# Two small maps made once on half of the matrix array, two groups of products moved in TensorE's order, and one load issued sooner

## The chip, the cores and the metric

The kernel runs on one core of a Trainium2 chip. A core has a matrix engine (TensorE, PE in the profile, with its weight loads as PEld), a vector engine (VectorE, DVE), a scalar engine (ScalarE, ACT), a general engine (GpSimd, POOL), and a queue engine that issues DMAs (SyncE, SP). The metric is the device time of one execution in microseconds (us), lower being better.

## The reference

x has 8 images of 256 channels and 64 x 64 pixels. Two layers follow each other, each of the form x + layer(group norm of x), with 32 groups of 8 channels.

Layer 0 computes, for every pixel, its own 3 x 3 filter:

```
x1, x2, x3 = 1x1 convolutions of gn(x): 32, 32 and 256 channels
h  = [x1, the 9 shifted copies of x2 (edge reflected)]      # 320 channels
h  = relu(bn(h));  h = relu(bn(cw1 h))                      # 32 channels
w  = cw2 h + cb2                                            # 9 taps for each of 32 groups
out[g, s] = sum over taps k of  w[g, k] * shift_k(x3[g, s]) # 8 channels s share a group's taps
```

Layer 1 adds two branches: an attention with 4 heads in which each pixel attends to its 7 x 7 neighbours (queries, keys with a position term, values, softmax over 49), and a dynamic convolution, in which x goes through two depthwise 3 x 3 convolutions for each of nine branches, and a softmax over the nine, from a 1x1 convolution of x, weights them.

## The kernel before

**Bands.** An image is cut into 8 bands of 8 rows (BAND = 512 pixels). Everything is done band by band, with channels or channel groups on the 128 partitions. One loop runs over g, from -12 to 63, and every g has 8 steps s. Step s does an eighth of layer 1's work on band g; beside it, layer 0 is done for a band 12 further on (AHEAD), since layer 1's normalisation needs a whole image of layer 0. While g is negative only layer 0 works: the *alone* stage, about 28 to 254 us of the profile. The rest, from 254 us on, is the *main* stage. In its last twelve bands, from about 3560 us, no layer 0 is left.

**Order.** The order of instructions on every engine is the order in which the program emits them (a manual schedule). A step has six places, each closed by `advance()`. `after(n, f)` emits f n places later. `steer` issues loads and starts chains of statistics. `beside(g, s)` returns two lists: `mid`, emitted behind the third place's beginning (the softmax's last scaling), and `end`, emitted behind the fifth. In the main stage a step puts on TensorE, in this order: weighted values of earlier scores (L735), scores (L691), the transposes of the probabilities before (ptp, L723), the first branch weights (pf, L813), what is in `mid`, the second pf, and what is in `end`.

**Buffers.** Results of TensorE lie in PSUM. Nearly all small users share the tag "gen" with five buffers, so that a group of matmuls waits until the buffer used five groups before has been emptied, mostly by ACT.

**Layer 0 for a band.** `small_maps` (called in `mid` of step 0) makes x1 and x2 from the loaded x (`xc`) with the scaled weights `w12s`: its 128 output partitions are x2 three times (one for each horizontal shift) and x1 once. Two products of 512 columns (L325) do it; in 32-bit floats each shows as two MATMULs. ACT copies them out, shifted by a column to each side (L332: three pieces of 32 partitions), with x1 (L335) and two reflected edge columns (L337, L338) into a tile of ten rows; POOL copies rows between neighbouring bands (L343 to L347). `value_maps` makes x3 (L357), copied out by ACT (L362) and stored to memory (L363) with two halves mt; in the main stage the first half is in `end` of step 0, the second in `mid` of step 1. `hidden_maps` starts a chain with the places `at`: hid for three vertical shifts t (ACT, L406), `conv` for t = 0 and 1, then for t = 2 (L417: 32-column products for four quarters of a band into `ph`), and a relu into h2n (ACT, L423). `tap_weights` makes three of the nine taps (pw, L435), and VectorE multiplies each with x3 rearranged by groups (`x3q`, loaded by L377, L381, L385): `prod`, L448. POOL adds the products to `xg` (x by groups, loaded by L393), L456; in the alone stage every third goes through TensorE instead (L469), and `combine` adds them on VectorE (L476). `take` takes statistics (L484) and stores the result x1 for layer 1 (L488).

**Statistics of the input.** `first_stats` loads x for bands of the next image into `xs`, a single buffer, at step 7, and takes its statistics (L283, VectorE) 16 places later in the alone stage, 9 later in the main stage. `scaled_weights` then makes w12s, w3s and, by products of one column (`through`), the biases.

**Dynamic sum.** `dynamic_sum` ends the dynamic convolution for a half of the channels: POOL adds two partial sums of exponentials (L824), VectorE takes reciprocals (L831 to L836), POOL multiplies and adds into `xr` (L841 to L843), and the band is stored.

Of the kernel before, what the change touches and what calls it, by code (L numbers as in the profile page):

```python
# [10 lines left out]
F32 = mybir.dt.float32  # L11
BF16 = mybir.dt.bfloat16
AF = mybir.ActivationFunctionType
# [5 lines left out]
P = 128  # L19
C = 256  # L20
NCT = C // P
H = W = 64
HW = H * W
R = 8
BAND = R * W
NB = H // R
# [4 lines left out]
REL = 32  # L31
# [29 lines left out]
AHEAD = NB + 4  # L61
AHEAD0 = AHEAD + NB + 1
# [24 lines left out]
def conv_layers_kernel(ctx: ExitStack, tc: tile.TileContext, ins: dict, out: bass.AP):  # L87
    nc = tc.nc
# [26 lines left out]
    par = load("par", [P, NPAR])  # L115
    chan = load("chan", [P, NCT, NCHAN], ins["chan"].rearrange("(t p) n -> p t n", p=P))
    rowp = load("rowp", [P, NROW], ins["rowp"].partition_broadcast(P))
    w12 = load("w12", [P, NCT, P], ins["w12"].rearrange("(t p) n -> p t n", p=P))
    w3 = load("w3", [P, NCT, C], ins["w3"].rearrange("(t p) n -> p t n", p=P))
    c1 = load("c1", [P, 3, REL])  # L120
    gq = load("gq", [P, P])
# [166 lines left out]
    def scaled_weights(b):  # L288

        im = images[b]  # L290

        def scale(sc, bi):
            im.w12s = w0.tile([P, NCT, P], F32, tag="w12s", name=f"w12s_{b}", bufs=1)
            im.w3s = w0.tile([P, NCT, C], F32, tag="w3s", name=f"w3s_{b}", bufs=1)
            for kt in range(NCT):
                nc.vector.tensor_scalar(im.w12s[:, kt], w12[:, kt], sc[:, kt : kt + 1], None, ALU.mult)
                nc.vector.tensor_scalar(im.w3s[:, kt], w3[:, kt], sc[:, kt : kt + 1], None, ALU.mult)
            after(5, lambda: through(bi))

        def through(bi):  # L300
            pb = ps.tile([P, 1 + NCT], F32, tag="gen", name=f"pb_{b}", bufs=5)
            for m, w in enumerate((w12, w3[:, :, :P], w3[:, :, P:])):
                for kt in range(NCT):
                    nc.tensor.matmul(
                        pb[:, m : m + 1], w[:, kt], bi[:, kt : kt + 1], start=(kt == 0), stop=(kt == NCT - 1)
                    )
# [12 lines left out]
    def small_maps(b, i):  # L319


        im = images[b]
        p12 = ps.tile([P, BAND], F32, tag="gen", name=f"p12_{b}_{i}", bufs=5)
        for kt in range(NCT):
            nc.tensor.matmul(p12, im.w12s[:, kt, :], im.xc[i][:, kt, :], start=(kt == 0), stop=(kt == NCT - 1))  # L325
        p12 = p12.rearrange("p (r c) -> p r c", r=R)
        t = im.x2[i] = w0.tile([P, HR, W], F32, tag="x2", name=f"x2_{b}_{i}", bufs=2)
        bias = im.bias
        for q, (dst, src) in enumerate(((1, 0), (0, 0), (0, 1))):
            n = W - (q != 1)  # L330
            s = slice(32 * q, 32 * q + 32)
            nc.scalar.activation(  # L332
                t[s, 1 : 1 + R, dst : dst + n], p12[s, :, src : src + n], AF.Identity, bias=bias[s, 0:1]
            )
        nc.scalar.activation(t[96:128, 0:R, :], p12[96:128], AF.Identity, bias=bias[96:128, 0:1])  # L335

        nc.scalar.activation(t[0:32, 1 : 1 + R, 0:1], p12[0:32, :, 1:2], AF.Identity, bias=bias[0:32, 0:1])  # L337
        nc.scalar.activation(  # L338
            t[64:96, 1 : 1 + R, W - 1 : W], p12[64:96, :, W - 2 : W - 1], AF.Identity, bias=bias[64:96, 0:1]
        )  # L340

        if i == 0:
            nc.gpsimd.tensor_copy(t[0:96, 0, :], t[0:96, 2, :])  # L343
        else:
            nc.gpsimd.tensor_copy(t[0:96, 0, :], im.x2[i - 1][0:96, R, :])
            nc.gpsimd.tensor_copy(im.x2[i - 1][0:96, R + 1, :], t[0:96, 1, :])
        if i == NB - 1:  # L347
            nc.gpsimd.tensor_copy(t[0:96, R + 1, :], t[0:96, R - 1, :])
# [471 lines left out]
    def dynamic_sum(b, i, ct, ex, oc):  # L820

        tot = ex[:, 1]
        xr = images[b].xr[i]
        nc.gpsimd.tensor_add(tot, tot, ex[:, 0])  # L824
        rec = w1.tile([P, BAND], F32, tag="rec", name=f"rec_{b}_{i}_{ct}", bufs=1)
        n = BAND // 2

        def quotient():


            nc.vector.tensor_scalar(tot, tot, 1.0, 1.0e37, ALU.add, ALU.min)  # L831
            nc.vector.reciprocal(rec[:, :n], tot[:, :n])
            after(3, second)

        def second():
            nc.vector.reciprocal(rec[:, n:], tot[:, n:])  # L836
            after(2, weigh)

        def weigh():

            nc.gpsimd.tensor_mul(tot, tot, rec)  # L841
            nc.gpsimd.tensor_mul(oc, oc, tot)
            nc.gpsimd.tensor_add(xr[:, ct], xr[:, ct], oc)  # L843
            if ct == NCT - 1:
                after(6, store)

        def store():
            nc.sync.dma_start(
                out=out[b].rearrange("(t p) n -> p t n", p=P)[:, :, i * BAND : (i + 1) * BAND], in_=xr
            )  # L850

        after(5, quotient)


    def beside(g, s):
# [51 lines left out]
        alone = g < 0  # L907
        if 0 <= g + AHEAD < B * NB:
            bq_, iq = divmod(g + AHEAD, NB)
            if s == 0:  # L910
                mid.append(lambda: small_maps(bq_, iq))
            if s == (2 if alone else 0):
                (mid if alone else end).append(lambda: value_maps(bq_, iq, 0))
            if s == (3 if alone else 1):
                mid.append(lambda: value_maps(bq_, iq, 1))
        if 0 <= g + AHEAD - 1 < B * NB and s == (2 if alone else 1):
            at = (3, 7, 8, 12, 16) if alone else (5, 9, 12, 15, 17)
            end.append(lambda: hidden_maps(*divmod(g + AHEAD - 1, NB), at))
        if 0 <= g + AHEAD - 2 < B * NB and s in TAPS_AT[alone]:
            u = TAPS_AT[alone].index(s)  # L920
# [5 lines left out]
    def steer(g, s):  # L926
# [4 lines left out]
        n = g + AHEAD + 1  # L931
        if s == 2 and n % NB == 0 and 0 < n < B * NB:
            scaled_weights(n // NB)
        if s == 7 and g + AHEAD0 < B * NB:
            first_stats(*divmod(g + AHEAD0, NB), n=16 if g < -1 else 9)
        if s == 5 and 0 <= g + 1 < B * NB:
            bn, inx = divmod(g + 1, NB)
            xr = images[bn].xr[inx] = x_tile("xr", bn, inx)
# [10 lines left out]
    with tc.manual_schedule():  # L949
# [21 lines left out]
        for g in range(-AHEAD, B * NB):  # L971
            b, i = divmod(g, NB)
            for s in range(STEPS):
                ct, m = divmod(s, NT // 2)
                mid, end = beside(g, s)
                steer(g, s)
                if g >= 0:
                    nm = f"{b}_{i}_{ct}_{m}"
                    sco = score_tile(nm)
                    weighted = [(a, weighted_values(*a, pt, sco)) for a, pt in pending]  # L980
# [53 lines left out]
def _layout(inputs):  # L1034
# [1 line left out]
    a = {k.replace("L0_conv_", "a_").replace("L1_conv_", "b_"): np.asarray(v) for k, v in inputs.items()}  # L1036
    f = np.float32
    arr = {"x": a["x"].reshape(a["x"].shape[0], C, HW)}
    arr["w12"] = np.concatenate([a["a_w2"].T] * 3 + [a["a_w1"].T], axis=1)
    arr["w3"] = a["a_w3"].T  # L1040

    def branch(v):
# [15 lines left out]
    par[:, PB21] = np.concatenate([a["a_b2"]] * 3 + [a["a_b1"]])  # L1058
# [55 lines left out]
```

## Time and profile before

| what | before |
|---|---|
| time, median of 3 runs | 4217.34 us (4215.47 to 4221.78) |
| the profiled execution | 4217.1 us |
| its span in the trace | 4215.3 us |
| mean TensorE clock granted | 0.994 of full |
| TensorE busy | 4079.7 us, 97% of the span |
| VectorE, ScalarE, GpSimd busy | 3582.1, 3046.5, 2900.3 us |
| x written by ACT (L332, L335, L337, L338): one | 670 and 679, 679, about 265 ns |
| VectorE waiting for xs in the alone stage | 47.3 us in 9 places |

A row of the profile's groups reads: line, engine, operation, output <- inputs with partitions x elements, count | busy us, mean ns of one | idle time of the engine just ahead of them, and what ended it. A group's mean can be longer than the time between two starts, since matmuls are pipelined; the distance from start to start is then what one costs. A row of the timeline reads: start, length, engine, line, operation, and for a run of equal instructions their count. A window reads: its bounds and length, and for each engine its busy time and count, then the clock granted to TensorE, the busy share of DMA and GB/s.

### The profile page before, as it was taken

The numbers are of one execution on the slowest core, as the hardware profiler recorded it, in microseconds if no ns is written. First come the engines' busy times: TensorE is split into PE (matmuls) and PEld (weight loads), VectorE is DVE, ScalarE is ACT, GpSimd is POOL, SyncE is SP. The second block draws the span as 40 slices with busy tenths as digits, with TensorE's granted clock in tenths as the row PEclk, the third lists the DMA queues.
The fourth block names the chain that finished last, engine by engine and source line by source line (L and its number), as shares of the span: only waits on it lengthen the run. The fifth ranks groups of instructions, "written<-read, shape, count | busy, mean of one in ns | idle before, by whom it ended". The sixth has DMA issues, their size and how long they took to land.

```text
span 4215.3 us, 72044 instructions
## 1 busy us (share of the span) xinstructions
PE 4079.7 (97%) x25004; PEld 2134.8 (51%) x25004; DVE 3582.1 (85%) x7244; ACT 3046.5 (72%) x7598; POOL 2900.3 (69%) x1778
## 2 busy tenths in 40 slices
PE   5889999999999999999999999999999999999998
PEld 2445555555555555555555555555555555555554
DVE  5778988888898898888988888888988888977777
ACT  3367778777777777877778777777778777677776
POOL 3657777677776777767777767767777777744445
PEclk9999999999999999999999999999999999999999
DMA  7753334233243333333333333343333233111100
GB/s 219 187 141 101 79 91 106 70 95 98 68 102 95 82 95 85 88 95 95 80 86 104 78 98 88 76 104 88 78 89 89 63 95 77 34 45 39 38 28 21
DMA packets 381260, 367.91 MB, mean 87 GB/s; under 512 B 55392, under 2 KB 282720, under 8 KB 380640
## 3 DMA queue, kind: packets, MB, share of 16 engines
q1 hardware_dynamic: 377568, 358.68, 33.4%
q8 instruction: 199, 3.26, 0.3%
q10 hardware_dynamic: 3328, 4.62, 0.3%
q14 instruction: 165, 1.35, 0.1%
HBM read 261.48 MB, written 101.71 MB: 86 GB/s over the span
## 4 chain that ended last, share of the span: by engine, by line
PE 74%; DVE 12%; POOL 7%; ACT 3%; issue 2%; SPq 2%; DMA 1%; POOLq 0%; ACTq 0%; DVEq 0%
PE pf L813 34%; PE ptp L723 6%; PE sco L735 5%; PE pk L646 5%; PE sco L691 5%; PE p L357 4%; POOL xg L456 4%; DVE prod L448 4%; PE pq L625 3%; PE pv L551 3%; PE pvt L595 2%; PE p L325 2%; PE pw L435 2%; POOL ex L1010 2%; DVE acc L796 2%
## 5 line engine op out<-in xcount | busy, mean ns | idle before, releaser
L813 PE MATMUL pf<-yp,c_wfc 128*128 128x512 f32 x4096 | 1932.4, 595 | 9.3 <-ACT vc L569 4.3
L456 POOL TENSOR_TENSOR xg<-xg,prod 128x1024 f32<-128x1024 f32 x549 | 1203.4, 2192 | 127.4 <-DVE prod L448 104.4
L813 PEld LDWEIGHTS pf<-yp,c_wfc 128*128 128x128 f32 x4096 | 733.8, 191 | 702.7 <-issue 658.9
L1010 POOL TENSOR_TENSOR ex<-ex,ex 128x1024 f32<-128x1024 f32 x384 | 907.7, 2364 | 61.9 <-ACT ex L818 57.2
L818 ACT ACTIVATE ex<-pf 128x512 f32<-128x512 f32 x1024 | 607.2, 593 | 335.7 <-PE pf L813 167.1
L770 DVE SCALAR_TENSOR_TENSOR acc<-yp,c_chan,acc 128x504 f32<-128x504 f32 (+3 forms) x1104 | 766.6, 694 | 47.7 <-ACT acc L761 27.1
L841 POOL TENSOR_TENSOR ex<-ex,rec 128x512 f32<-128x512 f32 x128 | 163.4, 1277 | 914.7 <-DVE rec L836 881.7
L796 DVE SCALAR_TENSOR_TENSOR acc<-hid,c_chan,acc 128x504 f32<-128x504 f32 (+3 forms) x1024 | 758.2, 740 | 20.2 <-ACT acc L790 2.1
L448 DVE SCALAR_TENSOR_TENSOR prod<-pw,c_par,x3q 128x1040 f32<-128x1040 f32 x576 | 734.4, 1281 | 46.3 <-PE pw L435 26.0
L717 ACT ACTIVATE prob<-prob,tot 128x196 f32<-128x196 f32 x1024 | 411.6, 450 | 467.9 <-DVE tot L715 467.9
L700 DVE CUSTOM_DVE_ANT_0 prob<-sco,c_mask 128x196 f32<-128x196 f32 x1024 | 325.1, 355 | 292.5 <-PE sco L691 292.0
L708 ACT ACTIVATE prob<-prob,nmax 128x196 f32<-128x196 f32 x1024 | 462.2, 456 | 46.9 <-DVE nmax L700 46.4
L735 PEld LDWEIGHTS sco<-pt,vt 112*64 112x64 f32 x8160 | 279.2, 137 | 209.5 <-issue 71.4
L723 PE MATMUL ptp<-ident,prob 128*112 128x128 f32 x2044 | 341.3, 287 | 26.4 <-ACT prob L717 25.9
L735 PE MATMUL sco<-pt,vt 112*64 112x64 f32 x8160 | 349.7, 228 | 0.0
L725 ACT COPY pt<-ptp 112x512 f32<-112x512 f32 x511 | 296.2, 580 | 70.5 <-PE ptp L723 66.5
L723 PEld LDWEIGHTS ptp<-ident,prob 128*112 128x112 f32 x2044 | 204.1, 133 | 194.0 <-ACT prob L717 69.4
L691 PE MATMUL sco<-kb,qb 64*64 64x196 f32 x4096 | 294.5, 357 | 0.2 <-DVE kb L661 0.2
L551 PE MATMUL pv<-yp,c_wv 128*128 128x512 f32 (+2 forms) x576 | 251.4, 561 | 0.0
L646 PE MATMUL pk<-yp,c_wk 128*128 128x512 f32 (+2 forms) x576 | 245.0, 552 | 0.0
L625 PE MATMUL pq<-yp,c_wq 128*128 128x512 f32 x512 | 242.2, 596 | 2.3 <-DVE prod L448 2.3
L357 PE MATMUL p<-xc,w3s 128*128 128x512 f32 x512 | 242.7, 598 | 0.0
(136 smaller groups left out, 5288.6 us busy)
## 6 DMA issues: line engine op xcount, KB each, us to landing
x<-x3n SPq DMA_DIRECT2D x128, 264.0 KB, 2.1
x3q<-x SPq DMA_DIRECT2D x128, 264.0 KB, 7.1
xc<-in_x SPq DMA_DIRECT2D x64, 512.0 KB, 5.0
xg<-in_x SPq DMA_DIRECT2D x256, 128.0 KB, 4.8
x<-xg SPq DMA_DIRECT2D x256, 128.0 KB, 2.4
yp<-x SPq DMA_DIRECT2D x128, 256.0 KB, 3.3
xr<-x SPq DMA_DIRECT2D x64, 512.0 KB, 5.7
out_x<-xr SPq DMA_DIRECT2D x64, 512.0 KB, 3.1
```

What stands on the lines that cost most here:

```text
L448: nc.vector.scalar_tensor_tensor(prod[:, :, :RUN], pw[:, j, :RUN].unsqueeze(1).to_broadcast([P, SHARE, RUN]), par[:, PCB2 + k : PCB2 + k + 1],
L456: nc.gpsimd.tensor_add(im.xg[i], im.xg[i], rows(prod))
L646: nc.tensor.matmul(pk[:, :n], wk[:, kt, ct * P : (ct + 1) * P], im.yp[i][:, kt, a : a + n], start=(kt == 0), stop=(kt == NCT - 1),)
L691: nc.tensor.matmul(sco[half[t], h, :NKEY], qb[half[h], 2 * m + t].rearrange("p r c -> p (r c)"), kb[half[h], :, c0 : c0 + KW], start=True, ...
L708: nc.scalar.activation(prob[:, h, :NKEY], prob[:, h, :NKEY], AF.Exp, bias=nmax[:, h : h + 1], scale=-1.0, accum_out=tot[:, h : h + 1],)
L723: nc.tensor.transpose(ptp[:, h, ch], prob[:, h, ch * CHUNK : (ch + 1) * CHUNK], ident)
L735: nc.tensor.matmul(po[half[h], :, t * TQ : (t + 1) * TQ], im.vt[i + ch, m][:n, t, (2 * ct + h) * HD : (2 * ct + h + 1) * HD], pt[:n, h, ch ...
L770: nc.vector.scalar_tensor_tensor(o, yp[:, ct, ra + dr : rb + dr, ca + dc : cb + dc], chan[:, ct, CW1 + k : CW1 + k + 1], o, ALU.mult, ALU.add,
L796: nc.vector.scalar_tensor_tensor(o, hid[:, ra + dr : rb + dr, ca + dc : cb + dc], chan[:, ct, CW2 + k : CW2 + k + 1], o, ALU.mult, ALU.add,)
L813: nc.tensor.matmul(pf, wfc[:, kt, 2 * m + j, ct * P : (ct + 1) * P], images[b].yp[i][:, kt, PAD : PAD + R], start=(kt == 0), stop=(kt == N ...
L818: nc.scalar.activation(ex[:, j].rearrange("p (r c) -> p r c", r=R), pf, AF.Exp)
L1010: after(4, lambda ex=ex, exb=exb: nc.gpsimd.tensor_add(ex, ex, exb))
```

## The change

The weights `w12` now hold w2 and w1 once, 64 columns. `small_maps` issues four products in place of two: each of 64 output partitions and 256 pixels, the upper four rows of the band on partitions 0 to 63 and the lower four on 64 to 127. ACT's writing out is a function of its own, `write_maps`: from each half, the three shifted copies of x2 and x1, 8 pieces of 252 or 256 elements; the two reflected edge columns are now copied by POOL out of the finished tile. In the main stage the products are issued at the beginning of step 0, just ahead of L735; the writing stays in `mid` of that step.

The places of `hidden_maps` in the main stage become (5, 13, 14, 19, 21): `conv` for t = 0, 1 moves from the middle of step 3 to its end, `conv` for t = 2 from the middle of step 4 to its end; hid for t = 2 and the relu are later as well.

In the alone stage the load of xs is issued at step 3 in place of step 7, and its statistics are taken 40 places later in place of 16, so at the place where they were. On SP's queue it now stands behind the stores of x1 and ahead of the loads of xg and x3q.

In the last band's second half, the four POOL operations of `dynamic_sum` go to VectorE.

```diff
-    w12 = load("w12", [P, NCT, P], ins["w12"].rearrange("(t p) n -> p t n", p=P))
+    w12 = load("w12", [P, NCT, 2 * REL], ins["w12"].rearrange("(t p) n -> p t n", p=P))
...
-            for m, w in enumerate((w12, w3[:, :, :P], w3[:, :, P:])):
+            for m, to, w in ((0, 0, w12), (0, 64, w12), (1, 0, w3[:, :, :P]), (2, 0, w3[:, :, P:])):
                 for kt in range(NCT):
                     nc.tensor.matmul(
-                        pb[:, m : m + 1], w[:, kt], bi[:, kt : kt + 1], start=(kt == 0), stop=(kt == NCT - 1)
+                        pb[to : to + w.shape[2], m : m + 1], w[:, kt], bi[:, kt : kt + 1],
+                        start=(kt == 0), stop=(kt == NCT - 1),
                     )
...
-        p12 = ps.tile([P, BAND], F32, tag="gen", name=f"p12_{b}_{i}", bufs=5)
+
+        p12 = ps.tile([P, R // 2, W], F32, tag="gen", name=f"p12_{b}_{i}", bufs=5)
         for kt in range(NCT):
-            nc.tensor.matmul(p12, im.w12s[:, kt, :], im.xc[i][:, kt, :], start=(kt == 0), stop=(kt == NCT - 1))
-        p12 = p12.rearrange("p (r c) -> p r c", r=R)
+            for u in range(2):
+                nc.tensor.matmul(
+                    p12[64 * u : 64 * u + 64], im.w12s[:, kt, :],
+                    im.xc[i][:, kt, u * BAND // 2 : (u + 1) * BAND // 2],
+                    start=(kt == 0), stop=(kt == NCT - 1),
+                )
+        return lambda: write_maps(b, i, p12)
+
+    def write_maps(b, i, p12):
+        im = images[b]
         t = im.x2[i] = w0.tile([P, HR, W], F32, tag="x2", name=f"x2_{b}_{i}", bufs=2)
         bias = im.bias
-        for q, (dst, src) in enumerate(((1, 0), (0, 0), (0, 1))):
-            n = W - (q != 1)
-            s = slice(32 * q, 32 * q + 32)
+        for u in range(2):
+            r, o = u * R // 2, 64 * u
+            for q, (dst, src) in enumerate(((1, 0), (0, 0), (0, 1))):
+                n = W - (q != 1)
+                nc.scalar.activation(
+                    t[32 * q : 32 * q + 32, r + 1 : r + 1 + R // 2, dst : dst + n],
+                    p12[o : o + 32, :, src : src + n], AF.Identity, bias=bias[o : o + 32, 0:1],
+                )
             nc.scalar.activation(
-                t[s, 1 : 1 + R, dst : dst + n], p12[s, :, src : src + n], AF.Identity, bias=bias[s, 0:1]
-            )
-        nc.scalar.activation(t[96:128, 0:R, :], p12[96:128], AF.Identity, bias=bias[96:128, 0:1])
-
-        nc.scalar.activation(t[0:32, 1 : 1 + R, 0:1], p12[0:32, :, 1:2], AF.Identity, bias=bias[0:32, 0:1])
-        nc.scalar.activation(
-            t[64:96, 1 : 1 + R, W - 1 : W], p12[64:96, :, W - 2 : W - 1], AF.Identity, bias=bias[64:96, 0:1]
-        )
+                t[96:128, r : r + R // 2, :], p12[o + 32 : o + 64], AF.Identity, bias=bias[o + 32 : o + 64, 0:1]
+            )
+
+        nc.gpsimd.tensor_copy(t[0:32, 1 : 1 + R, 0:1], t[0:32, 1 : 1 + R, 2:3])
+        nc.gpsimd.tensor_copy(t[64:96, 1 : 1 + R, W - 1 : W], t[64:96, 1 : 1 + R, W - 3 : W - 2])
...
-        nc.gpsimd.tensor_add(tot, tot, ex[:, 0])
+        engine = nc.vector if (b, i, ct) == (B - 1, NB - 1, NCT - 1) else nc.gpsimd
+        engine.tensor_add(tot, tot, ex[:, 0])
...
-            nc.gpsimd.tensor_mul(tot, tot, rec)
-            nc.gpsimd.tensor_mul(oc, oc, tot)
-            nc.gpsimd.tensor_add(xr[:, ct], xr[:, ct], oc)
+            engine.tensor_mul(tot, tot, rec)
+            engine.tensor_mul(oc, oc, tot)
+            engine.tensor_add(xr[:, ct], xr[:, ct], oc)
...
-            if s == 0:
-                mid.append(lambda: small_maps(bq_, iq))
+            if alone and s == 0:
+                mid.append(lambda: small_maps(bq_, iq)())
...
-            at = (3, 7, 8, 12, 16) if alone else (5, 9, 12, 15, 17)
+            at = (3, 7, 8, 12, 16) if alone else (5, 13, 14, 19, 21)
...
-        if s == 7 and g + AHEAD0 < B * NB:
-            first_stats(*divmod(g + AHEAD0, NB), n=16 if g < -1 else 9)
+        if s == (3 if g < -1 else 7) and g + AHEAD0 < B * NB:
+            first_stats(*divmod(g + AHEAD0, NB), n=40 if g < -1 else 9)
...
                 if g >= 0:
+                    if s == 0 and g + AHEAD < B * NB:
+                        mid.append(small_maps(*divmod(g + AHEAD, NB)))
```

The host lays out the weights and the bias column of w12 to match (w2 and w1 once; b2 and b1 twice).

More of the change, by code (lines that the diff above doesn't have):

```diff
@@ L292, in scale @@
         def scale(sc, bi):
-            im.w12s = w0.tile([P, NCT, P], F32, tag="w12s", name=f"w12s_{b}", bufs=1)
+            im.w12s = w0.tile([P, NCT, 2 * REL], F32, tag="w12s", name=f"w12s_{b}", bufs=1)
             im.w3s = w0.tile([P, NCT, C], F32, tag="w3s", name=f"w3s_{b}", bufs=1)
@@ L1038, in _layout @@
     arr = {"x": a["x"].reshape(a["x"].shape[0], C, HW)}
-    arr["w12"] = np.concatenate([a["a_w2"].T] * 3 + [a["a_w1"].T], axis=1)
+    arr["w12"] = np.concatenate([a["a_w2"].T, a["a_w1"].T], axis=1)
     arr["w3"] = a["a_w3"].T
@@ L1057, in _layout @@
         par[:, at : at + 3] = branch(a[f"a_bn1_{n}"])
-    par[:, PB21] = np.concatenate([a["a_b2"]] * 3 + [a["a_b1"]])
+    par[:, PB21] = np.concatenate([a["a_b2"], a["a_b1"]] * 2)
     for at, n in ((PG2, "g"), (PB2, "b"), (PM2, "m"), (PV2, "v")):
```

## The prediction

> **What bounds the kernel now.** I read the page's busy time and its chain first, then the windows of the three stages, then the matrix engine's timeline through one ordinary band, then the groups, and last the waits and the chain of the stage in which layer 0 runs alone. From the page (engine busy; then the chain that ended last):
>
> ```profile
> PE 4079.7 (97%) x25004; PEld 2134.8 (51%) x25004; DVE 3582.1 (85%) x7244; ACT 3046.5 (72%) x7598; POOL 2900.3 (69%) x1778
> ...
> PE 74%; DVE 12%; POOL 7%; ACT 3%; issue 2%; SPq 2%; DMA 1%; POOLq 0%; ACTq 0%; DVEq 0%
> ```
>
> The windows (stretch, then busy time of PE, PEld, DVE, ACT, POOL) say where this holds:
>
> ```profile
> 28.00:254.00 226.00, 174.43 (x759) 87.97 (x758) 158.26 (x181) 92.96 (x167) 145.19 (x90) 0.92 0.76 203
> 254.00:3560.00 3306.00, 3266.88 (x20223) 1714.35 (x20224) 2892.60 (x5844) 2479.28 (x6178) 2394.85 (x1453) 1.00 0.35 88
> ```
>
> From 254 us on TensorE is busy 3266.88 of 3306 us, so a microsecond of TensorE taken out there is worth one, unless something else then comes too late; VectorE, at 2892.60, is next (88%). Ahead of 254 us no engine is full. The timeline of TensorE (start, length, line) over the seam of two steps:
>
> ```profile
> 1594.85 0.60 PE L595 MATMUL pvt<-ident,vc 128*112 128x128 f32 x4
> 1595.28 1.88 PE L325 MATMUL p<-xc,w12s 128*128 128x512 f32 x4
> 1597.00 1.88 PE L813 MATMUL pf<-yp,c_wfc 128*128 128x512 f32 x4
> 1598.72 1.88 PE L357 MATMUL p<-xc,w3s 128*128 128x512 f32 x4
> 1600.53 0.69 PE L735 MATMUL sco<-pt,vt 112*64 112x64 f32 x16
> 1601.14 0.58 PE L691 MATMUL sco<-kb,qb 64*64 64x196 f32 x8
> ```
>
> Nothing is idle: each group starts before the modelled end of the last. From start to start, L325 costs 1.72 us (1595.28 to 1597.00), as does pf; but p of L357 ahead of L735 costs 1.81 us. I read the extra 0.09 as the price of a change of tile shape (full array to 64 columns). The groups by form:
>
> ```profile
> L735 PE MATMUL sco<-pt,vt 112*64 112x64 f32 x7664 | 342.5, 229 | 0.0
> ...
> L332 ACT ACTIVATE x<-p,bias 32x504 f32<-32x504 f32 x128 | 85.7, 670 | 49.8 <-PE p L325 49.0
> ...
> L338 ACT ACTIVATE x<-p,bias 32x8 f32<-32x8 f32 x64 | 17.0, 265 | 0.8
> ```
>
> Sixteen L735 of 229 ns each fit in 0.69 us: they overlap. Their records start in pairs, one per column half, 6 to 7 ns apart, pair after pair 58 ns, where 64 columns alone at L325's rate (429 ns for 512) are 54 ns. So two column halves run together at almost full rate. L417's four column quarters do it less well: 134 ns a round, against 107 for 128 columns.
>
> [...] here L843 takes 1273 ns on POOL, and VectorE's L476 1210 ns for twice the elements, about 2.1 times.
>
> **Half-width maps.** Two logical products of 512 columns with the full array (4 instructions by 429 ns, 1.72 us) become four of 256 columns on half the array, 8 instructions in 4 pairs. A pair at L325's rate is 215 ns, so 4 make 0.86; with L735's overhead of 4 ns a pair, 0.87 us. That is 0.85 us saved a band, in the 52 bands made from 254 us on: **44.1 us**. Bounds: with L417's overhead (25%) 1.07 us, 33.7 us saved; without overlap nothing. Put ahead of L735 they share its shape, 64 columns: the change of shape comes ahead of L325 in place of L735, so its 0.09 neither goes nor comes twice. Twelve bands fall in the alone stage, where TensorE waits; nothing there. The additional bias product per image and smaller weight scaling are below 0.2 us each: nothing.
>
> **Their evacuation.** ACT wrote 2 x 670 + 680 + 680 + 2 x 265 = 3.2 us; now 8 pieces of 252 or 256 elements. From 8 elements (265 ns) to 504 (670) the slope is 0.82 ns an element, so 252 cost 0.47, eight 3.7 us: 0.5 us more. ACT is at 75% in this stage, so this costs only if a buffer comes late. In this band the writes ended at 1600.9 and their PSUM buffer was wanted again by TensorE at 1603.86 (pvt of the next step), the one behind it (pf's) at 1604.29 after release at 1601.5: slack 3.0 and 2.8 us. Measured from the step's first L735: the scores come 0.87 later (the maps are now ahead of them), so softmax's ACT work and with it the writes do too; the step's end comes 0.85 earlier; the writes take 0.5 longer. About 0.7 and 0.6 us are left: no stall in an ordinary band, but I allow **2 us lost** in all for bands of which this isn't true (0 to 15 are possible). POOL's two edge copies are 0.23 each at most (L345's price) in place of ACT's 2 x 0.265; behind them stand the halo copies, wanted only at the end of the next step.
>
> **Inner maps' conv.** Each of its two parts stood between full-array products (pf, L417, pk or pv). Now it is the last group ahead of L735, where a change of shape is paid anyway: three changes become two, twice a band: 2 x 0.095 x 53 bands = **10.1 us**. In each image's first band L417 also waited for ACT's hid (7 times 0.86 from 254 us on): the third hid was issued at place 12 and its products at 15; now at 14 and 19, five places on: **6.0 us**. The relu comes 4 places later; its h2n is wanted only by the tap weights of the loop's next band, so I take nothing; were it late, PE would wait about the 0.48 us of that operation.
>
> **Statistics' x in the alone stage.** The chain in time:
>
> ```profile
> 94.25 1.14 DVE xg L476
> ...
> 104.95 0.61 SPq L385
> 105.60 5.21 DMA xs<-in_x
> ...
> 111.44 0.68 DVE st L283
> 112.12 1.20 DVE prod L448
> 113.32 1.14 DVE xg L476
> ```
>
> A band's loop is: combine, 16 issues on SP's queue (0.6 each), the landing of xs, statistics, a product, combine. The waits for xs sum to 47.3 us in 9 places. xs is now issued behind the four stores of x1, ahead of x3n, xg and x3q; its buffer is free by then. But the product behind the statistics needs the last piece of x3q, issued just ahead of xs before and last now, and xs's 512 KB go through ahead of it. Before, that piece landed 1.1 to 1.8 us ahead of xs (109.61 and 110.81; 128.89 and 130.73). With the same bytes on the same queue I expect it to land about where xs did. What leaves the loop is then only the statistics, 2 x 0.68 us, now done while x3q is on its way: 8 rounds by 1.3 to 1.4, **11 us**. Bounds: 5 if x3q lands later than xs did, 25 if it lands where it did before.
>
> **The last weighted sum.** Four operations of 1.26 on POOL become VectorE's, about 0.66 each (half of L476's 1210 and a little): 4 x 0.6 = **2.4 us**, all behind the last product, VectorE being idle there.
>
> **Sum.** 44.1 + 10.1 + 6.0 + 11 + 2.4 - 2 = 71.6 us. The profiled execution took 4217.1 us (span 4215.3 and 1.8 around it), 0.2 below the median of 4217.34; 4217.1 - 71.6 = 4145.5, I say **4145 us**. A change under about 0.2%, 8.4 us, could not be told from none.
>
> **Rivals.** *The halves don't overlap* (two streams of 256 columns need more than L735's 64 showed): the 44.1 go, 4189 us; against it, pairs in L735 6 ns apart. *VectorE becomes the bound*: 2892.60 of 3306 busy, and the waits of L723 for prob, 24.45 us in 44 places, all lie in a band's last two steps, where VectorE is already late; TensorE's time taken out of step 0 comes out of VectorE's idle 2.78 us of step 1, which covers it in ordinary bands. If half of the 54 us of the first and third edits turn into such waits, 4172. *The wait for xs goes whole*, because x3q lands where it did: 14 more, 4131. *Slower*: the fixed part of a narrow write is larger than 8 elements show. The writes fit 3.7 + 0.6 us. At 0.72 us a piece they take 5.75, TensorE waits 1.4 us in step 1 of each of 52 bands, and all gain is gone; from 0.76 on, 4230. Against it, 128x196 writes on ACT take 450 to 456 ns and 32x8 265.
>
> **How the numbers follow.** The forecast as worked out 0.70, with its own range 4132 to 4158; xs's wait gone whole 0.10; VectorE 0.09; no overlap 0.07; slower 0.04. The two far cases are left out of the range for the most part: 4126 to 4174. Faster 0.95 (all but the slower case and a sliver), within 0.2% 0.02, slower 0.03.
>
> **What would show it.** Groups of the new maps of 0.87 us from start to start, with L735 behind them at once; eight narrow writes of 0.47; L417's new form ahead of L735 without its wait on hid; in the alone stage VectorE's statistics waiting for no DMA, its product waiting for x3q instead; in the tail VectorE where POOL stood. Wrong would make it: waits on ACT at pvt or p in step 1, longer waits of L723 for prob, or maps of 1.7 us.

## The result

The changed kernel takes 4152.41 us (median of 4 runs, 4151.30 to 4159.20) against 4217.48 for the kernel before (4 runs, 4215.47 to 4221.78): a ratio of 0.9848, 95% interval 0.9831 to 0.9865, 65 us. The profiled execution took 4152.64 us, its span 4150.9. The forecast was 4145. The page of the changed kernel (engine busy, then the chain that ended last):

```profile
PE 4022.6 (97%) x25292; PEld 2126.8 (51%) x25292; DVE 3591.9 (87%) x7248; ACT 3081.0 (74%) x7726; POOL 2923.0 (70%) x1902
...
PE 71%; DVE 14%; POOL 6%; ACT 5%; DMA 2%; issue 2%; SPq 1%; POOLq 0%; ACTq 0%; DVEq 0%
```

TensorE has lost 57 us of busy time, VectorE none, so VectorE's share rose from 85% to 87% and its part of the chain from 12% to 14%. The windows (stretch, busy time of PE, PEld, DVE, ACT, POOL, clock, DMA share, GB/s):

```profile
28.00:254.00 226.00, 179.72 (x840) 88.17 (x836) 164.70 (x195) 105.54 (x206) 150.78 (x114) 0.90 0.87 210
254.00:3560.00 3306.00, 3264.61 (x20825) 1738.08 (x20825) 2949.42 (x5940) 2544.42 (x6375) 2465.81 (x1584) 1.00 0.36 89
```

The first window now reaches 8 us into the main stage, whose first scores start at 246.30 us and not at 254.10. In the second, TensorE is as full as it was (3264.61 of 3306), and does more work in the same stretch. The timeline of TensorE over the seam of the same two steps as in the prediction:

```profile
1561.67 0.60 PE L607 MATMUL pvt<-ident,vc 128*112 128x128 f32 x4
1562.20 1.08 PE L328 MATMUL p<-xc,w12s 128*64 128x256 f32 x8
1563.11 0.64 PE L747 MATMUL sco<-pt,vt 112*64 112x64 f32 x16
1563.68 0.57 PE L703 MATMUL sco<-kb,qb 64*64 64x196 f32 x8
...
1566.39 0.60 PE L607 MATMUL pvt<-ident,vc 128*112 128x128 f32 x4
1566.82 1.88 PE L825 MATMUL pf<-yp,c_wfc 128*128 128x512 f32 x4
1568.54 1.88 PE L369 MATMUL p<-xc,w3s 128*128 128x512 f32 x4
```

The maps (L328) take 0.91 us from start to start, where L325 took 1.72. The weighted values behind them (L747) take 0.57 where 0.62 was usual: after a change of shape the second pair of a group starts about 0.05 us late (0.107 us after the first where L747 stands behind L369, 0.060 behind the maps), and now that falls to the maps (0.267, where their further pairs are 0.215 apart). Together 0.86 us for the maps: the forecast had 0.87. ACT's writes (groups by form):

```profile
L343 ACT ACTIVATE x<-p,bias 32x252 f32<-32x252 f32 x256 | 118.0, 461 | 44.4 <-PE p L328 37.0 <-DMA c_wk<-in_wk 5.0
```

461 ns a piece, against 470 forecast. I then took, for every step of every band, the time from its scores to those of the next step, and the difference to the kernel before. The medians by the image's band (bands 2 and 4 are like band 1), in us a step (the seam moves 0.86 from step 0 to step 7, since the maps are now ahead of the first scores):

```
band   step 0     1      2      3      4      5      6      7    whole band
  0    -0.98   0.00   0.00  -0.20  -1.13   0.25   0.30   0.86    -0.89
  1    -1.72   0.00   0.00  -0.20  -0.20   0.00   0.13   0.86    -1.11
  3    -1.72   0.00   0.00  -0.20  -0.20   0.09   0.64   0.86    -0.52
  5    -1.72   0.00   0.00  -0.20  -0.20   0.00   0.12   0.87    -1.11
  6    -1.72   0.00   0.00  -0.20  -0.19   0.37   0.00   0.86    -0.89
  7    -2.01   0.00   0.00  -0.20  -0.20   0.01   0.00   0.86    -1.53
```

Over 52 bands, steps 3 and 4 give 27.0 us, and steps 5 and 6 take 13.5 back. The rest of the 65: the first scores come 7.8 us sooner (8.7 without the maps that are now ahead of them), and from the last scores to the end of the span it is 19.4 us in place of 21.7. So the table raises two questions that the forecast did not raise: why moving the conv gave 0.4 us a band and not 0.2, and what takes it back in steps 5 and 6.

### The profile page after: what moved, and what is told of

It reads as the page before. It is cut to its first block, busy times and chain, and to the rows that moved or that the text cites. A ratio compares the mean times of both kernels' runs of the same rounds, so it can differ in the third digit from the quotient of the medians.

```text
span 4150.9 us, 72735 instructions
## 1 busy us (share of the span) xinstructions
PE 4022.6 (97%) x25292; PEld 2126.8 (51%) x25292; DVE 3591.9 (87%) x7248; ACT 3081.0 (74%) x7726; POOL 2923.0 (70%) x1902
## 4 chain that ended last, share of the span: by engine, by line
PE 71%; DVE 14%; POOL 6%; ACT 5%; DMA 2%; issue 2%; SPq 1%; POOLq 0%; ACTq 0%; DVEq 0%
PE pf L825 33%; PE ptp L735 5%; PE sco L747 5%; PE pk L658 5%; PE sco L703 5%; PE p L369 5%; DVE prod L460 4%; PE pq L637 4%; POOL xg L468 3%; PE pvt L607 2%; PE pv L563 2%; DVE acc L808 2%; PE pw L447 2%; DVE acc L782 2%; POOL ex L1026 2%
## 5 line engine op out<-in xcount | busy, mean ns | idle before, releaser
L825 PE MATMUL pf<-yp,c_wfc 128*128 128x512 f32 x4096 | 1930.5, 595 | 10.6 <-ACT vc L581 5.0
L782 DVE SCALAR_TENSOR_TENSOR acc<-yp,c_chan,acc 128x504 f32<-128x504 f32 (+3 forms) x1104 | 766.2, 694 | 42.3 <-ACT acc L773 21.7
L747 PEld LDWEIGHTS sco<-pt,vt 112*64 112x64 f32 x8160 | 283.8, 137 | 182.3 <-issue 51.7
L735 PE MATMUL ptp<-ident,prob 128*112 128x128 f32 x2044 | 341.7, 287 | 31.2 <-ACT prob L729 30.5
L747 PE MATMUL sco<-pt,vt 112*64 112x64 f32 x8160 | 347.0, 227 | 0.0
L735 PEld LDWEIGHTS ptp<-ident,prob 128*112 128x112 f32 x2044 | 203.9, 133 | 201.4 <-issue 77.7
L369 PE MATMUL p<-xc,w3s 128*128 128x512 f32 x512 | 244.4, 601 | 0.0
```

What stands on the lines that cost most here:

```text
L369: nc.tensor.matmul(p3, im.w3s[:, kt, mt * P : (mt + 1) * P], im.xc[i][:, kt, :], start=(kt == 0), stop=(kt == NCT - 1),)
L735: nc.tensor.transpose(ptp[:, h, ch], prob[:, h, ch * CHUNK : (ch + 1) * CHUNK], ident)
L747: nc.tensor.matmul(po[half[h], :, t * TQ : (t + 1) * TQ], im.vt[i + ch, m][:n, t, (2 * ct + h) * HD : (2 * ct + h + 1) * HD], pt[:n, h, ch ...
L782: nc.vector.scalar_tensor_tensor(o, yp[:, ct, ra + dr : rb + dr, ca + dc : cb + dc], chan[:, ct, CW1 + k : CW1 + k + 1], o, ALU.mult, ALU.add,
L825: nc.tensor.matmul(pf, wfc[:, kt, 2 * m + j, ct * P : (ct + 1) * P], images[b].yp[i][:, kt, PAD : PAD + R], start=(kt == 0), stop=(kt == N ...
```

## The experiments

**Each part alone.** Three kernels: the half-width maps alone, the moved conv alone (the line with `at` in the kernel before), and the sooner load of xs alone.

```diff
 # conv_only, in the kernel before
-            at = (3, 7, 8, 12, 16) if alone else (5, 9, 12, 15, 17)
+            at = (3, 7, 8, 12, 16) if alone else (5, 13, 14, 19, 21)
 # xs_only, in the kernel before
-        if s == 7 and g + AHEAD0 < B * NB:
-            first_stats(*divmod(g + AHEAD0, NB), n=16 if g < -1 else 9)
+        if s == (3 if g < -1 else 7) and g + AHEAD0 < B * NB:
+            first_stats(*divmod(g + AHEAD0, NB), n=40 if g < -1 else 9)
 # maps_only: the changed kernel with these two, and the engine of the last dynamic sum, put back
```

> The kernel before with the half-width maps alone (made ahead of weighted values, written out in the old place). If TensorE's time saved is passed on: 52 bands by 0.855 us (914 ns for the maps and 50 ns less for the weighted values behind them, against 1719) less some 4 us of waits for buffers in step 0, so about 40 us faster, 4177 us. If the waits for VectorE in a band's steps 5 to 7 already eat the gain of this edit by itself: 30 us faster or less, 4188 or more.

> The kernel before with the moved conv alone. The prediction's own count (one change of shape less a part, 0.095 each, and no wait for hid): 16 us faster, 4201. If going from 32 columns to 64 costs nothing, as the trace of the changed kernel suggests, two changes go for each part, 0.2 us: 21 us and 6.5 for the wait, less what comes back as waits for VectorE in steps 5 and 6; 20 to 27 us faster, 4190 to 4197.

> The kernel before with the sooner load of xs in the alone stage alone. If the last piece of x3q now lands where xs landed and only the statistics leave the loop: 9 us faster, 4208. If the wait for the transfer were really shorter: 20 us or more, 4197 or less.

Measured, beside a kernel before of 4216.80:

| kernel | median us | ratio, 95% interval | change |
|---|---|---|---|
| maps alone | 4174.24 | 0.9901 (0.9888 to 0.9915) | -42.6 |
| conv alone | 4203.22 | 0.9969 (0.9957 to 0.9981) | -13.6 |
| xs alone | 4209.88 | 0.9983 (0.9977 to 0.9990) | -6.9 |

With the 2.3 us of the tail these make 65.4, the whole change 65.1: the parts add up, each being known to within some 3 to 6 us. The maps are passed on whole except in each image's first band (the section on the prediction shows why); their step 6 differs from the kernel before by -1.0 us over all bands, so they cause no lateness there. The conv alone is outside what I expected from the trace (20 to 27), and nearer to the first count of 16, but for another reason. Over 52 bands its steps 3 and 4 are 27.0 us shorter in sum, its steps 5 and 6 are 16.2 longer. Why steps 3 and 4 gave twice the forecast stands in the timeline of the kernel before, image's band 3:

```profile
2005.60 1.88 PE L813 MATMUL pf<-yp,c_wfc 128*128 128x512 f32 x4
2007.41 0.43 PE L417 MATMUL ph<-hid,c_c 96*32 96x128 f32 x8
2007.77 1.98 PE L551 MATMUL pv<-yp,c_wv 128*128 128x512 f32 x4
2009.59 1.88 PE L813 MATMUL pf<-yp,c_wfc 128*128 128x512 f32 x4
...
2013.00 1.88 PE L813 MATMUL pf<-yp,c_wfc 128*128 128x512 f32 x4
2014.72 1.88 PE L551 MATMUL pv<-yp,c_wv 128*128 128x512 f32 x4
2016.44 1.88 PE L813 MATMUL pf<-yp,c_wfc 128*128 128x512 f32 x4
```

Start to start, pf ahead of L417 takes 1.81 us, and pv *behind* L417 takes 1.82, where pv without a change takes 1.72. So each way costs about 0.1: going into a narrower shape is seen on the group ahead, coming back to the full array on the group behind. In its new place nothing is added for it: pf ahead of L735 paid its 0.09 there already, and L735 follows L417 at no visible cost (0.36 us for L417's eight and 0.615 for L735, as elsewhere). What takes it back in step 6 is seen one step on in the same band. The kernel before:

```profile
2020.88 0.57 PE L691 MATMUL sco<-kb,qb 64*64 64x196 f32 x8
2021.38 0.65 PE L723 MATMUL ptp<-ident,prob 128*112 128x128 f32 x4
2022.77 1.99 PE L813 MATMUL pf<-yp,c_wfc 128*128 128x512 f32 x4 [0.73 <-ACT vc L569]
```

and with the conv moved alone:

```profile
2010.94 0.58 PE L691 MATMUL sco<-kb,qb 64*64 64x196 f32 x8
2011.89 0.78 PE L723 MATMUL ptp<-ident,prob 128*112 128x128 f32 x4 [0.37 <-ACT prob L717]
2013.55 1.98 PE L813 MATMUL pf<-yp,c_wfc 128*128 128x512 f32 x4 [0.88 <-ACT vc L569]
```

The wait has grown from 0.73 to 1.25 us in two places. ACT's vc of L569 is queued behind its prob (L717), and that, in both kernels, behind VectorE's reciprocal of the sums. ACT's row, first of the kernel before:

```profile
2020.59 0.81 ACT L717 ACTIVATE prob<-prob,tot 128x196 f32<-128x196 f32 x2 [2.65 <-DVE tot L715]
```

and with the conv moved:

```profile
2011.38 0.81 ACT L717 ACTIVATE prob<-prob,tot 128x196 f32<-128x196 f32 x2 [2.28 <-DVE tot L715]
```

Before, prob began 0.29 us ahead of the step's scores, now 0.44 behind them: VectorE kept its own time while TensorE came sooner, and TensorE then waited for it. Band 3 loses most in step 6 (0.73 us in the median); an ordinary band loses 0.11 to 0.17.

xs alone: the product now waits for x3q, as forecast, but x3q is later than xs had been. VectorE's timeline in the alone stage, first of the kernel before:

```profile
110.83 1.29 DVE L283 BATCH_NORM_STATS2 st<-xs 128x6 f32<-128x512 f32 x2 [2.77 <-DMA xs<-in_x]
112.03 1.28 DVE L448 SCALAR_TENSOR_TENSOR prod<-pw,c_par,x3q 128x1040 f32<-128x1040 f32 x1
```

and with the sooner xs alone:

```profile
105.29 1.28 DVE L283 BATCH_NORM_STATS2 st<-xs 128x6 f32<-128x512 f32 x2
111.77 1.30 DVE L448 SCALAR_TENSOR_TENSOR prod<-pw,c_par,x3q 128x1040 f32<-128x1040 f32 x1 [5.21 <-DMA x3q<-x]
```

In the kernel before xs landed at 110.81; now the piece of x3q that ends the product's wait lands at 111.50 (before, the same piece at 109.26). The product starts 0.26 us sooner here, not 1.3.

**Where the maps stand.**

```diff
-            if alone and s == 0:
+            if s == 0:
                 mid.append(lambda: small_maps(bq_, iq)())
...
-                    if s == 0 and g + AHEAD < B * NB:
-                        mid.append(small_maps(*divmod(g + AHEAD, NB)))
```

> The changed kernel with the half-width maps in their old place in the middle of step 0 (between full-array products). If a change of shape costs 0.095 to 0.10 us each way and weighted values then pay their own again: 52 bands by 0.2 to 0.25 us, 10 to 13 us slower than the changed kernel, 4162 to 4165; but the scores no longer come 0.9 us later in step 0, so some 4 us of waits for buffers there can come back: 4158 to 4165. If the place decided nothing: 4152.

4171.37 us (0.9897, 0.9883 to 0.9910): 19 us slower than the changed kernel, more than I had put. Its timeline of TensorE over the same work:

```profile
1573.94 0.60 PE L607 MATMUL pvt<-ident,vc 128*112 128x128 f32 x4
1574.47 1.08 PE L328 MATMUL p<-xc,w12s 128*64 128x256 f32 x8
1575.48 1.98 PE L825 MATMUL pf<-yp,c_wfc 128*128 128x512 f32 x4
1577.30 1.88 PE L369 MATMUL p<-xc,w3s 128*128 128x512 f32 x4
```

pvt takes 0.53 (0.44 without a change behind it), the maps 1.01 (0.91), pf 1.82 (1.72), and the weighted values later pay their 0.05 again. A detour from the full array to half of it and back is thus 0.09 + 0.10 + 0.10 + 0.05 = 0.34 us. The steps agree: 0.35 us a band, about 16 over the 45 bands that aren't an image's first, and step 6 is 3.6 longer over all bands; in the first bands it is only 0.1, since the changed kernel waits there for ACT. Put ahead of L735, the maps add no change of shape that the step had not. So of the 42.6 us of the half-width maps, the place makes almost half.

**The order of the halves.**

```diff
-        for kt in range(NCT):
-            for u in range(2):
+        for u in range(2):
+            for kt in range(NCT):
```

> The changed kernel with the order of the four products turned: both of the first half, then both of the second, so that neighbours in the queue use the same column half. If only neighbours on different halves overlap, 8 instructions by some 215 ns minus one overlapping pair: maps of 1.5 to 1.7 us in place of 0.91, 52 by 0.6 to 0.8, 31 to 42 us slower than the changed kernel, 4184 to 4194. If the engine overlaps further apart: 4152.

4155.57 us (0.9852, 0.9838 to 0.9865), the changed kernel's time. The maps still take 0.91 us from start to start; the second of a pair merely starts 13 to 14 ns after the first, where it was 6 to 8. Eight instructions one after another at 0.215 us each (half of L325's 0.43 for 512 columns) would take 1.72, so the halves still overlap. The records don't say which half one works on; in the program's order a product is two instructions, so partners stand four places apart here, where the changed kernel has them two apart.

**One tap less.** This kernel leaves one of nine taps out of the first depthwise convolution of the second half of the channels.

```diff
-            ks = [k for k in range(KK) if k != 4 and taps(...)[0] < taps(...)[1]]
+            ks = [k for k in range(KK - ct) if k != 4 and taps(...)[0] < taps(...)[1]]
```

> The changed kernel without one of the nine taps of the first depthwise convolution for the second half of the channels (VectorE, 0.69 us, in step 5): this leaves a term out of the result. Nothing changes on TensorE or ScalarE. If the waits of transposes for prob in steps 5 to 7 come from VectorE being late there, they shrink by up to 0.7 us where they are that long (first, fourth, sixth band of an image and a little in the others): 10 to 20 us faster than the changed kernel, 4132 to 4142. If ScalarE or PSUM buffers set them: within 3 us of 4152.

4121.25 us (0.9775, 0.9761 to 0.9788): 31 us faster than the changed kernel, more than expected. An operation of 0.7 us that is VectorE's alone is worth 0.78 us in step 7 of the image's bands 0, 1, 2, 4 and 5, and nothing there in bands 3, 6 and 7: 26.6 us of the 31. The tap stood behind the reciprocal L727 in step 5, and the waits in step 6 did not change; those in step 7, which the kernel before had too, went. TensorE's waits, first of the changed kernel:

```profile
PE ptp L735 <- ACT prob L729: 30.5, 56, 2.7
```

and without the tap:

```profile
PE ptp L735 <- ACT prob L729: 18.9, 21, 2.7
```

ScalarE's work is unchanged, so VectorE's work in these steps sets this wait.

**Tap products in other steps.**

```diff
-TAPS_AT = (1, 3, 5), (0, 2, 4)
+TAPS_AT = (0, 2, 4), (0, 2, 4)
```

> The changed kernel with layer 0's tap products started in steps 0, 2 and 4 in place of 1, 3 and 5 in the main stage, so that six of VectorE's nine products leave steps 4, 6 and 7 for steps 1, 2, 3 and 5, where it waits for scores. If VectorE is late in steps 5 to 7 for its products: 10 us or more faster than the changed kernel, 4142 or less. If it is late in any order, since 89% of its time is taken: 4150 to 4155; and slower if step 5 with two products is worse than step 6 with two.

4433.07 us (1.0512, 1.0497 to 1.0526), 281 us slower than the changed kernel, far outside of what I expected. In the changed kernel L727 of step 1 came 4.95 us after the step's scores; here a product stands ahead of it too, the addition of one (L845) takes 1.81 us in place of 0.42, and L727 begins 0.30 us after the next step's scores. Steps 2, 3 and 7 are longer by 1.6, 1.2 and 2.9 us in the median. A part of this goes with a lower clock: in 40 places from the first scores on, 27 of them in step 7 of bands 1, 2, 4 and 5, the granted TensorE clock stands at half for 3.4 us (in the changed kernel in 2 places); estimated from these 3.4 us, that is at most 1.7 us each. The idle time that VectorE shows ahead of the scores was room for late work, not free to be filled ahead of L727.

**VectorE's addition of one.** In step 5 one VectorE instruction is much longer than in step 1 (0.42 us). The changed kernel's VectorE:

```profile
1540.70 0.34 DVE L757 SCALAR_TENSOR_TENSOR xr<-sco,bv,xr 128x128 f32<-128x128 f32 x1
1541.53 2.38 DVE L845 TENSOR_SCALAR ex<-ex 128x512 f32<-128x512 f32 x1 [0.48 <-POOL ex L838]
1543.94 1.75 DVE L846 RECIPROCAL rec<-ex 128x256 f32<-128x256 f32 x1
1545.61 1.45 DVE L782 SCALAR_TENSOR_TENSOR acc<-yp,c_chan,acc 128x504 f32<-128x504 f32 x2
1546.97 0.16 DVE L727 RECIPROCAL tot<-tot 128x2 f32<-128x2 f32 x1
```

and its GpSimd:

```profile
1541.45 2.17 POOL L468 TENSOR_TENSOR xg<-xg,prod 128x1024 f32<-128x1024 f32 x1
```

GpSimd's addition started 0.08 us ahead of it and ended at 1543.62; VectorE's ended 0.3 later. The others go the same way: of the changed kernel's 128 additions of one, the 49 that start while a GpSimd instruction runs, all in step 5, end 0.28 us after it (in band 5, where a fill of x3q follows it on GpSimd, 0.28 after that); the other 79 take 0.41 to 0.43 us. What the 49 take above that I call the hold-up; why they end with GpSimd's, no run shows. It is 2.0 us in bands 0, 1, 2 and 4, 2.4 in band 5, 0.5 and 1.2 in bands 6 and 7, none in band 3, and 1.3 in the mean of step 5. In band 3, the one shown for the moved conv, the weights scaled for the next image are held instead; the changed kernel's VectorE:

```profile
1975.39 1.25 DVE L296 TENSOR_SCALAR w12s<-c_w,sc_a 128x64 f32<-128x64 f32 x1
1976.57 2.32 DVE L297 TENSOR_SCALAR w3s<-c_w,sc_a 128x256 f32<-128x256 f32 x1
```

and its GpSimd:

```profile
1975.23 1.36 POOL L838 TENSOR_TENSOR ex<-ex 128x512 f32<-128x512 f32 x1
1976.56 2.18 POOL L468 TENSOR_TENSOR xg<-xg,prod 128x1024 f32<-128x1024 f32 x1
```

They end 0.05 and 0.15 us after these; with no GpSimd instruction beside them, at 25 us, such rows take 0.25 and 0.35 us. The bands in which one tap less was worth 0.78 us are those held for 2 us or more: that fits with the hold-up making VectorE late there, and doesn't show it. I tried to take the addition from VectorE; `one` is a column of ones, and the clamp at 1e37 that the same instruction makes is left out:

```diff
-            nc.vector.tensor_scalar(tot, tot, 1.0, 1.0e37, ALU.add, ALU.min)
+            nc.scalar.activation(tot, tot, AF.Identity, bias=one)
```

> The changed kernel with the addition of one in the dynamic sum (L845, VectorE) made by ScalarE in the same place of the order; the clamp at 1e37 that the same instruction made is left out. In step 5 that instruction takes 2.38 us in the trace, 0.42 in step 1; in step 5 it lies under a tensor addition of GpSimd. If this hold-up makes VectorE late in steps 5 to 7: VectorE is 2.4 us ahead there, all the waits of transposes for prob go, 30 to 45 us faster than the changed kernel, 4107 to 4122. If VectorE only waits elsewhere, or ScalarE's additional 0.6 us twice a band decides: 4145 to 4160.

> As the run before, with the inner maps' conv in the old places. If VectorE's lateness is what took the conv's gain back, that gain is now whole: 0.4 us a band by 53 bands and the 6.5 us of waits for hid, so 24 to 28 us slower than with the conv moved. If something else took it: 12 to 15 us slower, as for the conv's move alone.

> Both found gains together on the changed kernel: ScalarE's addition of one, and xs loaded in step 2 of the alone stage. The stages don't overlap, so the gains should add up: 10 us faster than with ScalarE's addition alone, 4097 to 4112.

4274.42 us (1.0135, 1.0121 to 1.0149) with ScalarE's addition; 4284.04 with the conv put back too (1.0156, 1.0140 to 1.0171); 4257.71 with the sooner xs instead (1.0097, 1.0083 to 1.0111). All are slower than the kernel before: the expectations failed. In an ordinary band (4), ScalarE now waits 1.1 us for GpSimd's sum in step 5 with all that is queued behind it, and the first reciprocal begins no sooner after the scores than before (4.5 us in both). In step 1, where nothing had held the addition, that reciprocal now begins 5.3 us after the scores in place of 1.9 (medians). Steps 2, 3 and 6 are 48, 26 and 23 us longer over all bands. So the wait wasn't taken away, but put where more waits behind it. Putting the conv back cost 10 us here and not 24 to 28, and even these are not the conv's for the most part: in bands 1 to 5 and 7 steps 3 and 4 lose 0.4 us and step 6 gives 0.4 back, to within 0.05 us in the median, and the trace's loss lies in the first bands (0.5 us each) and in band 6 (2.0 us in four of six), where in these four the granted clock stands at half for 3.4 us. These three neither show nor refute what the hold-up is worth; the third shows a gain for xs of 17, from a kernel whose alone stage was itself slower (first scores at 254.03 us, where the changed kernel has 246.30).

**The reciprocal of the sums first.** Last, the order in step 5: L845 and L846 two places later, so that L727 comes ahead of them, and xs as in the next experiment.

```diff
-            after(3, second)
+            after(1, second)
...
-        after(5, quotient)
+        after(7, quotient)
```

> The kernel with xs loaded in step 2 of the alone stage (4142), and the dynamic sum's addition of one and first reciprocal (VectorE, L845 and L846, together 4.1 us in step 5) two places later, behind the reciprocal of the attention's sums (L727) in place of ahead of it; second reciprocal and GpSimd's products stay in their places. If VectorE's order in step 5 is what makes ScalarE's prob, and all that ScalarE has behind it, late in steps 6 and 7: the time that the conv's move gave back there (15 us) returns, and part of the waits that were there before it: 15 to 40 us less than 4142, 4102 to 4127. If VectorE's sum of work decides: 4137 to 4147, or slower where the reciprocals come later for GpSimd.

4152.90 us (0.9849, 0.9836 to 0.9863), 10.6 slower than the kernel with the sooner xs alone. VectorE's timeline of that kernel in step 5:

```profile
1535.31 1.52 DVE L782 SCALAR_TENSOR_TENSOR acc<-yp,c_chan,acc 128x504 f32<-128x504 f32 x2
1536.74 0.16 DVE L727 RECIPROCAL tot<-tot 128x2 f32<-128x2 f32 x1
1537.52 2.38 DVE L845 TENSOR_SCALAR ex<-ex 128x512 f32<-128x512 f32 x1 [0.63 <-POOL ex L838]
```

L727 is 4.6 us sooner after its scores. Step 6 becomes 24.8 us shorter over 52 bands, by 0.2 us in ordinary bands and 1.6 in bands 0 and 3: the waits that the moved conv had met there are gone, so it was VectorE's order in step 5 that set them. But step 7 becomes 29.6 us longer and step 3 9.0. VectorE's sum of work in steps 4 to 7 stays, the hold-up included (2.38 us in the row above), and I take it that what isn't waited for in step 6 is waited for in step 7; no run shows this apart from what else the new order does to step 7.

**xs another step sooner.**

```diff
-        if s == (3 if g < -1 else 7) and g + AHEAD0 < B * NB:
-            first_stats(*divmod(g + AHEAD0, NB), n=40 if g < -1 else 9)
+        if s == (2 if g < -1 else 7) and g + AHEAD0 < B * NB:
+            first_stats(*divmod(g + AHEAD0, NB), n=46 if g < -1 else 9)
```

> The changed kernel with xs loaded yet a step sooner in the alone stage, ahead of the stores of x1 too. If the loop is held by the transfers' bytes (DMA 87% busy in the stage): within 3 us of 4152. If by where xs stands ahead of x3q on SP's queue, its bytes then flow while the stores wait for their data: 5 to 15 us faster.

4142.31 us (0.9822, 0.9809 to 0.9836), 10 us faster than the changed kernel, which is the second of the two cases. xs now stands ahead of the stores of x1, for whose data SP's queue waits 13.6 us in 7 places of the changed kernel's alone stage, and no longer between them and x3q; that it goes through during these waits is my reading of the order. Eight rounds of the alone stage, combine to combine, take 161.6 us in the kernel before, 155.9 with xs alone, 155.6 in the changed kernel and 146.7 here. VectorE's waits in the alone stage, of the changed kernel:

```profile
DVE prod L460 <- DMA x3q<-x: 18.8, 6, 7.5
DVE st L283 <- DMA xs<-in_x: 15.9, 2, 12.1
```

and of this one:

```profile
DVE prod L460 <- DMA x3q<-x: 12.7, 5, 9.5
DVE prod L460 <- POOL xg L468: 10.2, 10, 2.1
DVE st L283 <- DMA xs<-in_x: 9.6, 1, 9.6
```

The transfers' bytes are the same in both, so it was their order and not their amount that cost these 10 us.

## Why the prediction was right, and where it wasn't

The direction and the time (4152 in a range of 4126 to 4174) were right, and so was the bound: TensorE. By its own sum:

| step | forecast us | measured us | from |
|---|---|---|---|
| half-width maps, with 2 lost to waits | 42.1 | 42.6 | maps alone |
| conv and its wait for hid | 16.1 | 13.6 | conv alone |
| xs in the alone stage | 11 | 6.9 | xs alone |
| last sum on VectorE | 2.4 | 2.3 | last scores to end of span |
| all | 71.6 | 65.1 | medians |

*Half-width maps.* The overlap read from L735's pairs held for 256 columns (0.86 us against 0.87), and the rival without overlap is out. The narrow writes cost 0.46, not 0.72, so the slower rival's threshold was not reached. The slack of 0.6 us behind the writes sufficed: step 1 is unchanged (0.00) in all bands of the table. The 2 us that the forecast allowed for it were lost, but elsewhere and as 5: in step 0 of an image's first band, which gave 0.98 in place of 1.72, 0.7 us by 7. Its pvt, first in the kernel before and then in the changed one:

```profile
772.66 0.60 PE L595 MATMUL pvt<-ident,vc 128*112 128x128 f32 x4
```

```profile
755.74 0.27 PE L607 MATMUL pvt<-ident,vc 128*112 128x128 f32 x1
756.17 0.54 PE L607 MATMUL pvt<-ident,vc 128*112 128x128 f32 x3 [0.16 <-ACT vc L581]
```

Before, the maps stood ahead of it for 1.72 us, while ACT copied vc. Now pvt takes 0.37 us longer, waiting for vc, and pv, 5 us ahead of it, starts 0.26 late, behind ACT's copy vt (L609), and takes 0.1 longer. ACT does both ahead of the maps' writes, so it isn't their length that costs. That the last band of an image gave 0.3 more was not forecast either.

*Inner maps' conv.* The size of two steps was wrong, and the errors cancelled: that 13.6 is near 16.1 is luck. "Three changes become two" with 0.095 for the one that goes (in the kernel before, pf takes 1.813 us ahead of L417 and 1.717 to 1.720 ahead of a full-array group): both the way in and the way back go, 0.2 us for each part, and steps 3 and 4 gave 20.5 us in place of 10.1, with 6.5 for hid as forecast (6.0). Then half of it was lost: the prediction had VectorE as a rival with 0.09 and let the time saved in step 0 come "out of VectorE's idle 2.78 us of step 1". That holds for what is saved in step 0, as the maps alone show, but not for time saved in steps 3 and 4, behind that idle time and right ahead of the steps where VectorE is already late. The waits of L723 were named and not applied to the edit that stands just ahead of them. The 16.2 us in steps 5 and 6 of the conv alone are that term.

*xs.* The statistics left the loop as forecast, and x3q took xs's place as the thing waited for; it lands 0.7 us later than xs did in the round shown, not in the same place, and so the loop gained 0.7 us a round (5.7 over eight) and not 1.3. It is inside the bounds of 5 and 25, near their lower end.

*Last sum.* VectorE's four operations take 0.69 us each, 0.66 was estimated:

```profile
4144.87 0.69 DVE L855 TENSOR_TENSOR ex<-ex,rec 128x512 f32<-128x512 f32 x1
```

What stays open: what VectorE's hold-up in step 5 costs. The one kernel that took the instruction away changed the waits of two other engines with it.

## What to carry to other kernels

When an edit takes time from the bounding engine, ask in which stretch, and which other engine has idle time *behind* that stretch and ahead of the next wait: 0.86 us taken in step 0 was passed on whole in all bands but an image's first, 0.4 us in steps 3 and 4 by half. Look too at what the moved work had hidden in its old place: in the first band ACT's copy of vc was no longer covered. Count a change of the array's tile shape on both sides, on the group ahead and on the group behind (0.09 and 0.10 us here), and look for a neighbour of like shape first: the place of the maps made 19 us of the 42.6 that all that was done to them gave. And ask what a load that is moved ahead of others on a queue makes late: xs ahead of x3q had x3q's piece land at 111.50 us in place of 109.26, and one step sooner, ahead of the stores for whose data the queue had waited 13.6 us, it gave 10 us more.

## What the runs showed of the hardware that was not expected

Two column halves of TensorE overlapped in both orders tried, with partners two and four places apart in the program (0.91 us for the maps both ways). Going from the full array to 32 or 64 columns costs 0.09 us on the group ahead, coming back 0.10 on the group behind, and for the 64-column maps another 0.10 on themselves (1.01 us in place of 0.91). Going from 32 columns to 64 adds nothing visible beyond this: the first group in a 64-column shape starts its second pair 0.05 us late, behind 32 columns as behind the full array. VectorE's addition of a constant, 128x512 in place, takes 0.42 us alone and 2.37 to 2.39 in the 30 places where a GpSimd tensor addition of 128x1024 starts 0.07 to 0.09 us ahead of it and no fill follows that, ending 0.28 to 0.29 us after it; the reciprocals and multiply-adds near it keep their usual times (1.75 us for a reciprocal of 256, 0.75 for a multiply-add of 504, with a GpSimd instruction beside them or without). GpSimd's two copies of 32x8 take 188 and 284 ns, where one of 96x64 takes 231 to 234: the small size bought nothing.
